# Loading and splitting the first x of a cross-attention kernel in another way, with the bias of the values taken off TensorE and the last pieces put on alternating banks

## The chip, the cores and the metric

The kernel runs on one core of one Trainium2 chip. The metric is the device time in microseconds (us) of one execution. Shown for the kernel before are the median of three runs and one further execution that was profiled.

## What is computed

For each of 32 batches, `x` and `y` (called `ctx_2048` outside) are arrays of 256 channels by 1024 positions in float32; the weights are 256x256. Cut to what matters:

```python
x_q = einsum('oc,bcn->bno', w_qk, y)
x_k = einsum('oc,bcn->bon', w_qk, x)
x_v = einsum('oc,bcn->bon', w_v, x) + b_v[None, :, None]
energy = einsum('bnc,bcm->bnm', x_q, x_k)
attention = softmax(energy, axis=-1)
attention = attention / (1e-07 + attention.sum(axis=1, keepdims=True))
x_r = einsum('bcn,bnm->bcm', x_v, attention)
x_r = relu(einsum('oc,bcn->bon', w_t, x - x_r) + b_t[None, :, None])
return x + x_r
```

## The kernel before, in words

**Arithmetic.** Every large product is made of three products of rounded float32 numbers: an operand is held as a HIGH form, a LOW form and a REST form (`FORMS`, line 210), and a left form is multiplied with its matching right form. So a product for 128 output channels and 512 columns is six matmuls of 128x512 (two blocks of input channels, three forms). Both query and key weights are folded into one matrix `gw` (w_qk times itself), and w_t and w_v into `vw`. So the program first makes `gw` (`square` and `weights`, lines 721 to 752), the transposed w_t (`turn_w`, line 798), from it `tw` and `vw` (`value_weights`, line 820), and a few bias vectors (`biases`, line 827).

**Work of a batch.** `keys` multiplies `gw` with the forms `xf` of x and leaves the forms `gf`; `values` (V) multiplies `vw` with `xf`, turns the result with VectorE into the tile `turned`, sends it through DRAM (`blocks`) and back into `yr` or `turned`, and makes the forms `uf` from it; `straight` (W) multiplies `tw` with `xf` and leaves `xe`; `energy` (E0 to E7) multiplies the forms `yf` of y with `gf`, takes a minimum on VectorE, an exponential on ScalarE, and leaves the forms `ef` and the running sum `acc`; `attention` (A0 to A7) multiplies `uf` with `ef`. The LOW form of `ef` is the last one to be ready: GpSimd adds it up from two parts (line 527). `sums` and `finish` divide, add and store. The last batch has an ending of its own, `ready_end`, `divided`, `beside` and `end` (lines 595 to 673): there W is added into the same banks as the attention, and VectorE takes it out of them in pieces that are stored at once.

**First batch.** x of batch 0 comes into `xr` by four DMAs of 128 partitions by 512 columns (lines 701 and 702), two on SyncE's queue and two on ScalarE's. `first_x(h)` (line 754) makes the forms of one half of the columns: for the first 128 channels ScalarE copies HIGH and VectorE makes REST and LOW; for the other 128 VectorE (first half) or GpSimd (second half) copies HIGH, GpSimd makes REST and VectorE makes LOW. `first_keys` (tokens fH00 and so on: form, block of channels k, half of the columns h) gives two matmuls of the first keys.

**Order.** TensorE's order is written out by hand as strings of tokens (lines 167 to 181): `SET_UP`, `FIRST` for batch 0, `STEADY`, `BEFORE` and `LAST`. In them `z` is one idle product on the tile `few`, `x0` and `x1` a call of `first_x`, G, T, Q and b the four weight steps, y the first two loads of y. The orders of all other engines, and of the DMAs on SyncE's and ScalarE's queues, come out of the class `Plan` (lines 17 to 163). It knows for each operation an engine, a length, a delay, what it reads and writes and whether it holds the SBUF access that VectorE and GpSimd have in common (`port`); it tries four variants (`LOOKS`) of a list schedule and emits that with the shortest span by its own numbers. A changed length or a changed string can so move instructions anywhere in the program. The program waits for a DMA by one of eight lanes taken in turn; a DMA that takes a lane which is still in use waits for it on the engine that issues it.

All computing instructions carry line 231 of the profile, since a helper records them; they are told apart by their tiles.

Of the kernel before, what the change touches and what calls it, by code (L numbers as in the profile page):

```python
# [184 lines left out]
def kernel(  # L185
# [513 lines left out]
    half = [ts(h, MB) for h in range(MH)]  # L699
    load(["wqk0", "wqk1"], 2.7, [(wqk[:, k], w_qk[ts(k, P)]) for k in range(KC)])  # L700
    load(["xr00", "xr10"], 6.0, [(xr[:, k, half[0]], x[0, ts(k, P), half[0]]) for k in range(KC)])
    load(["xr01", "xr11"], 7.4, [(xr[:, k, half[1]], x[0, ts(k, P), half[1]]) for k in range(KC)])
    load(["wt0", "wt1"], 8.3, [(wt[:, k], w_t[ts(k, P)]) for k in range(KC)])
    load(["wv0", "wv1"], 9.2, [(wv[:, k], w_v[ts(k, P)]) for k in range(KC)])
# [245 lines left out]
```

## Time and profile before

| What | Value |
| --- | --- |
| median of three runs | 1937.68 us (1937.02 to 1938.92) |
| the profiled execution's own time | 1936.26 us |
| its span, first to last instruction | 1934.5 us |
| TensorE busy | 1926.5 us, 8500 matmuls |
| VectorE, ScalarE, GpSimd busy | 1493.8, 1474.2, 1549.4 us |
| instructions | 24348 |
| first values product of batch 0 starts | 18.38 us |
| first attention product of batch 0 starts | 40.83 us |

The profiled execution lies 1.76 us over its span and 1.42 us under the median of the runs. PE stands for TensorE's matmuls, PEld for its weight loads, DVE for VectorE, ACT for ScalarE, POOL for GpSimd; SPq and ACTq are instructions that issue a DMA. In a timeline row come the start and the length in us, the engine, the operation with what it writes and reads, the shape, and how many such instructions in a row are merged; in square brackets stands the idle time before them and what ended it. TensorE's matmuls are pipelined: the distance from one start to the next tells their rate, not the length of one.

### The profile page before, as it was taken

What the parts mean: (1) busy time and instruction counts of PE and PEld (TensorE: products, weight loads), DVE (VectorE), ACT (ScalarE), POOL (GpSimd) and SP (SyncE); (2) the same over time, 40 slices, a digit from 0 to 9 for tenths busy, and PEclk for the clock granted to TensorE, in tenths of its full rate; (3) what the DMA queues carried; (4) which work ended last, traced back from release to release, by engine and by line L of the source; (5) the groups of instructions that cost most, each with busy time, mean ns of one, the idle gap of its engine ahead of it and who ended that gap; (6) DMA issues with size and microseconds to landing.
All of it is one profiled execution on the core that took longest, in us unless ns stands there. A gap on an engine that the chain in (4) does not pass through costs nothing.

```text
span 1934.5 us, 24348 instructions
## 1 busy us (share of the span) xinstructions
PE 1926.5 (100%) x8500; PEld 1593.5 (82%) x8500; DVE 1493.8 (77%) x2107; ACT 1474.2 (76%) x1929; POOL 1549.4 (80%) x775
## 2 busy tenths in 40 slices
PE   9999999999999999999999999999999999999998
PEld 7888888888888888888888888888888888888887
DVE  7777787787777877778777777777787777877777
ACT  6778777788777887777977778777787777887775
POOL 5788877888778888787887878877888778887777
PEclk9999999999999999999999999999999999999999
DMA  6675666666666657666575675666656666667642
GB/s 181 141 175 149 177 164 147 147 160 167 173 147 149 160 160 179 144 153 159 157 176 145 149 172 144 184 156 147 156 153 174 167 149 143 162 164 177 158 102 77
DMA packets 128779, 301.76 MB, mean 156 GB/s; under 512 B 12944, under 2 KB 47248, under 8 KB 128656
## 3 DMA queue, kind: packets, MB, share of 16 engines
q1 hardware_dynamic: 92256, 200.19, 33.4%
q0 software_dynamic: 35680, 99.10, 29.2%
q8 instruction: 67, 1.10, 0.2%
q10 hardware_dynamic: 720, 0.92, 0.1%
q14 instruction: 56, 0.46, 0.1%
HBM read 167.25 MB, written 67.11 MB: 121 GB/s over the span
## 4 chain that ended last, share of the span: by engine, by line
PE 99%; DVE 1%; issue 0%; DVEq 0%; ACT 0%
PE banks L231 99%; DVE xf L231 0%; DVE z L231 0%; DVE banks L231 0%; DVE gw L231 0%; DVE xe L231 0%; DVEq L945 0%; ACT gw L231 0%; DVE few L231 0%; DVE nbias L231 0%; DVE ubias L231 0%
## 5 line engine op out<-in xcount | busy, mean ns | idle before, releaser
L231 POOL TENSOR_TENSOR ef<-ef 128x1024 fp32r<-128x1024 f32 x256 | 619.5, 2421 | 140.4 <-DVE acc L231 59.4
L231 PE MATMUL banks<-gf,yf 128*128 128x512 f32 x3072 | 727.6, 389 | 0.0
L231 PE MATMUL banks<-ef,uf 128*128 128x512 f32 x3072 | 727.2, 389 | 0.0
L231 PEld LDWEIGHTS banks<-gf,yf 128*128 128x128 f32 x3072 | 576.3, 188 | 120.7 <-DVE ef L231 0.6
L231 PEld LDWEIGHTS banks<-ef,uf 128*128 128x128 f32 x3072 | 576.8, 188 | 119.6
L231 DVE SCALAR_TENSOR_TENSOR ef<-banks,small,ef 128x512 fp32r<-128x512 f32 x512 | 369.9, 743 | 59.1 <-ACT ef L231 56.9
L231 DVE TENSOR_REDUCE small<-banks 128x1 f32<-128x1024 f32 x256 | 312.2, 1220 | 131.9 <-PE banks L231 131.9
L231 ACT ACTIVATE ef<-banks,small 128x512 fp32r<-128x512 f32 x512 | 337.4, 688 | 12.4 <-DVE acc L231 1.2
L231 ACT ACTIVATE banks<-banks,small 128x1024 f32<-128x1024 f32 x256 | 278.4, 1088 | 81.4 <-DVE small L231 80.8
L231 DVE SCALAR_TENSOR_TENSOR acc<-banks,small,acc 128x512 f32<-128x512 f32 x448 | 317.4, 744 | 5.5
L231 ACT ACTIVATE gf<-banks 128x1024 fp32r<-128x1024 f32 x64 | 65.7, 1029 | 307.3 <-PE banks L231 307.3
L231 ACT ACTIVATE ef<-ef 128x1024 fp32r<-128x1024 f32 x256 | 270.9, 1059 | 1.1
L231 POOL TENSOR_TENSOR z<-z,xe 128x1024 f32<-128x1024 f32 (+1 forms) x64 | 150.8, 2373 | 107.3 <-DVE z L231 104.9
L231 POOL TENSOR_TENSOR uf<-yr,uf 128x1024 fp32r<-128x1024 f32 x64 | 153.6, 2400 | 48.5 <-ACT uf L231 48.5
L231 PE MATMUL banks<-xf,gw 128*128 128x512 f32 x768 | 186.1, 390 | 1.8 <-DVE xf L231 1.7
L231 PE MATMUL banks<-xf,tw 128*128 128x512 f32 (+1 forms) x774 | 184.9, 388 | 0.8 <-DVE z L231 0.6
L231 PE MATMUL banks<-xf,vw 128*128 128x512 f32 x768 | 184.7, 389 | 0.0
L231 PEld LDWEIGHTS banks<-xf,gw 128*128 128x128 f32 x768 | 143.7, 188 | 32.7 <-DVE xf L231 1.5
L231 PEld LDWEIGHTS banks<-xf,tw 128*128 128x128 f32 x774 | 144.6, 188 | 31.1 <-DVE z L231 0.8
L231 PEld LDWEIGHTS banks<-xf,vw 128*128 128x128 f32 x768 | 144.1, 188 | 30.3 <-DVE ef L231 0.3
L231 POOL TENSOR_TENSOR xf<-xr,xf 128x1024 fp32r<-128x1024 f32 (+1 forms) x64 | 151.0, 2382 | 6.2 <-DVE xf L231 6.2
L231 POOL TENSOR_TENSOR uf<-turned,uf 128x1024 fp32r<-128x1024 f32 x64 | 155.2, 2424 | 0.0
(69 smaller groups left out, 1573.3 us busy)
## 6 DMA issues: line engine op xcount, KB each, us to landing
yr<-in_ctx_dram SPq DMA_DIRECT2D x64, 512.0 KB, 3.9
blocks<-turned SPq DMA_DIRECT2D x256, 128.0 KB, 2.7
yf<-in_ctx_dram POOLq DMA_DIRECT2D x63, 512.0 KB, 6.1
yf<-yf POOLq DMA_DIRECT2D x63, 512.0 KB, 6.6
xr<-in_x_dram SPq DMA_DIRECT2D x62, 512.0 KB, 3.8
xo<-in_x_dram SPq DMA_DIRECT2D x62, 512.0 KB, 4.5
xf<-xf POOLq DMA_DIRECT2D x62, 512.0 KB, 5.8
out_dram<-z SPq DMA_DIRECT2D x62, 512.0 KB, 4.5
```

Of the source, the lines that this page charges most:

```text
L231: self.last = getattr(self.engine, name)(*args, **kwargs)
```

## The change

Four things are changed.

1. x of batch 0 is loaded by blocks of 128 channels: each block is two DMAs of 64 partitions by 1024 columns, one on each of the two queues. In both kernels these DMAs are issued between those of w_qk and those of w_t. `first_x(k)` takes a block of channels instead of a half of the columns; ScalarE copies HIGH, and VectorE makes REST and LOW, for both blocks. GpSimd has no part in it any more.
2. The product of w_t and b_v (eight matmul passes with one column, on the path of `biases`) is dropped from TensorE. b_v is loaded into all 128 partitions (128 KB written instead of 1 KB), GpSimd multiplies it with w_t, and VectorE sums the rows up.
3. In `end`, the last block of channels of the last batch is made in four groups of 256 columns that go to the two banks in turn, instead of one of 512 columns and two of 256 on one bank.
4. The strings `SET_UP` and `FIRST` are written anew, some lengths given to the planner too, y's first load gets an earlier due time, and a copy of one column on ScalarE is put ahead, so that ScalarE's table is loaded there.

```diff
 SET_UP = (
-    "x1 z G z z x0 z fH10 y fH00 fR10 T fH01 fL10 b fR01 fR00 fL01 Q fL00 fH11 fL11 fR11"
+    "z z z x0 z G T x1 fH00 fR00 fH01 fR01 fL00 Q fL01 fH11 fH10 fL10 y b fR11 fR10 fL11"
 FIRST = (
-    "V0^ W1^ E0 E1 V1^ W0^ X E2 E3 A0 A1 E4 E5 A2 A3 E6 E7 A4 Y2 A5 Y3 v0 A6 S k0 A7 k1 O"
+    "V0^ V1^ W1^ E0 E1^ W0^ E2 E3 X A0 A1 E4 E5 Y2 A2 A3 E6 E7 A4 Y3 A5 v0 A6 k1 S A7 O k0"
...
-        by_sync(5.8 if q else 7.8, [], ["yr"], lambda: sync.dma_start(r, from_))
+        by_sync(5.8 if q else 7.3, [], ["yr"], lambda: sync.dma_start(r, from_), early=0.0 if q else 45.0)
...
-        for h in range(MH):
-            cuts = [(0, MB)] if not last or h != MH - 1 else [(0, MB // 2), (MB // 2, MB)]
-            for lo, hi in cuts:
+        cuts = [(0, MB)] if not last else [(0, MB // 2), (MB // 2, MB)]
+        for lo, hi in cuts:
+            for h in range(MH):
...
-    load(["xr00", "xr10"], 6.0, [(xr[:, k, half[0]], x[0, ts(k, P), half[0]]) for k in range(KC)])
-    load(["xr01", "xr11"], 7.4, [(xr[:, k, half[1]], x[0, ts(k, P), half[1]]) for k in range(KC)])
+    for k, landing in enumerate((4.4, 5.8)):
+        load(
+            [f"xr{k}0", f"xr{k}1"], landing,
+            [(xr[ts(q, P // 2), k], x[0, k * P + q * (P // 2) : k * P + (q + 1) * (P // 2)]) for q in range(2)],
+        )
...
+    plan.add("act", 1.3, 0.0, ["few"], ["acc0"], lambda: act.copy(acc[:, :1], few[:, :1]), early=59.0)
...
-    def first_x(h):
-        at = ts(h, MB)
-        for k in range(KC):
+    def first_x(k):
+        raw_names = [f"xr{k}{q}" for q in range(2)]
+        for h in range(MH):
...
-                if k == 0:
-                    on_act(MB, [f"xr{k}{h}"], nh, lambda: act.copy(high, raw))
-                elif h == 0:
-                    dve_in_sbuf(MB // 2, [f"xr{k}{h}"], nh, lambda: dve.tensor_copy(high, raw))
-                else:
-                    on_pool(MB // 2, [f"xr{k}{h}"], nh, lambda: pool.tensor_copy(high, raw))
-                add = dve_in_sbuf if k == 0 else on_pool
-                on = dve if k == 0 else pool
-                add(
-                    MB, [f"xr{k}{h}"] + nh, nr,
-                    lambda: on.tensor_tensor(rest, raw, value(high), ALU.subtract),
-                )
+                on_act(MB, raw_names, nh, lambda: act.copy(high, raw))
+                dve_in_sbuf(MB, raw_names + nh, nr, lambda: dve.tensor_tensor(rest, raw, value(high), ALU.subtract))
...
-        by_sync(6.8, [], ["bv"], lambda: sync.dma_start(bv, b_v.rearrange("(k p o) -> p k o", p=P, o=1)))
+        by_sync(6.6, [], ["bv"], lambda: sync.dma_start(bvs, b_v.partition_broadcast(P)))
...
-        plan.add("pe", 0.45, 0.163, ["wtT", "bv", "z1", "acc0", "acc1"], ["wtb", "bank7"], product)
+        on_pool(
+            KC * C, ["wt0", "wt1", "bv", "z0", "z1"], ["wqk0", "wqk1"],
+            lambda: pool.tensor_tensor(each, wt, bvs.unsqueeze(1).broadcast_to([P, KC, C]), ALU.mult),
+        )
 
         def of():
+            dve.tensor_reduce(nbias[:, :, 0], each, AX.X, ALU.add)
```

TensorE's rows at the start of the program before (`few` are the idle products, `z` with 256 columns is G, `z` with 128 columns is T, `xf,gw` are the first keys, `z,acc` is the bias product, `acc,z` is Q, `xf,vw` V, `xf,tw` W, `gf,yf` E):

```order
L231 MATMUL banks<-few 128x128 x6
L231 MATMUL banks<-z 128x256 x4
L231 MATMUL banks<-few 128x128 x3
L231 MATMUL banks<-xf,gw 128x512 x6
L231 MATMUL banks<-z 128x128 x4
L231 MATMUL banks<-xf,gw 128x512 x4
L231 MATMUL banks<-z,acc 128x1 x4
L231 MATMUL banks<-xf,gw 128x512 x6
L231 MATMUL banks<-acc,z 128x256 x4
L231 MATMUL banks<-xf,gw 128x512 x8
L231 MATMUL banks<-xf,vw 128x512 x12
L231 MATMUL banks<-xf,tw 128x512 x12
```

The same place on TensorE now:

```order
L231 MATMUL banks<-few 128x128 x9
L231 MATMUL banks<-z 128x256 x4
L231 MATMUL banks<-z 128x128 x4
L231 MATMUL banks<-xf,gw 128x512 x10
L231 MATMUL banks<-acc,z 128x256 x4
L231 MATMUL banks<-xf,gw 128x512 x14
L231 MATMUL banks<-xf,vw 128x512 x24
L231 MATMUL banks<-xf,tw 128x512 x12
```

All nine idle products now stand ahead of G, T ahead of all 24 matmuls of the first keys, Q behind ten of them, and the second values product (V1) directly behind the first.

VectorE's rows behind the two memsets before, up to the last step of `vw` (`xe<-banks,gw` and `xe<-banks,vw` are intermediate results of `weights`; `xf` are the forms of x):

```order
L231 SCALAR_TENSOR_TENSOR xe<-banks,gw 128x256 x2
L231 SCALAR_TENSOR_TENSOR gw<-banks,gw 128x256
L231 CAST xf<-xr 128x512
L231 SCALAR_TENSOR_TENSOR gw<-banks,gw 128x256
L231 TENSOR_TENSOR xf<-xr,xf 128x512
L231 SCALAR_TENSOR_TENSOR xf<-xf 128x512
L231 TENSOR_TENSOR xf<-xr,xf 128x512
L231 SCALAR_TENSOR_TENSOR xf<-xf 128x512 x2
L231 TENSOR_SCALAR ubias<-banks 128x2
L231 TENSOR_TENSOR nbias<-banks,z 128x2
L231 TENSOR_SCALAR xbias<-nbias 128x2
L231 SCALAR_TENSOR_TENSOR xf<-xf 128x512
```

VectorE's rows there now, with the steps of `vw` that stand between and behind:

```order
L231 TENSOR_TENSOR xf<-xr,xf 128x512
L231 SCALAR_TENSOR_TENSOR xf<-xf 128x512 x2
L231 TENSOR_TENSOR xf<-xr,xf 128x512
L231 SCALAR_TENSOR_TENSOR xe<-banks,gw 128x256
L231 SCALAR_TENSOR_TENSOR xf<-xf 128x512
L231 TENSOR_TENSOR xf<-xr,xf 128x512
L231 SCALAR_TENSOR_TENSOR gw<-banks,gw 128x256
L231 SCALAR_TENSOR_TENSOR xe<-banks,vw 128x256
L231 SCALAR_TENSOR_TENSOR xf<-xf 128x512
L231 SCALAR_TENSOR_TENSOR xe<-banks,vw 128x256
L231 SCALAR_TENSOR_TENSOR vw<-banks,vw 128x256 x2
```

Three rows of `gw` and `xf` stand ahead of these (`xe<-banks,gw`, a TENSOR_TENSOR on `xf`, `gw<-banks,gw`). So VectorE has eight steps on `xf` instead of seven, the steps of `gw` and `vw` stand between them, and the bias rows are gone from here: they follow 4 rows behind, among the steps of `gf`.

VectorE's rows in a batch from the middle of the program, from E0's minimum on (TENSOR_REDUCE on `small`) to the second half of `ef` of E1, before:

```order
L231 TENSOR_REDUCE small<-banks 128x1 x2
L231 RECIPROCAL small<-small 128x1
L231 TENSOR_SCALAR acc<-banks,small 128x512 x2
L231 RECIPROCAL small<-small 128x1
L231 SCALAR_TENSOR_TENSOR ef_80<-banks,small,ef_80 128x512
L231 SCALAR_TENSOR_TENSOR acc<-banks,small,acc 128x512
L231 TENSOR_REDUCE small<-banks 128x1
L231 SCALAR_TENSOR_TENSOR ef_80<-banks,small,ef_80 128x512
L231 SCALAR_TENSOR_TENSOR acc<-banks,small,acc 128x512
L231 SCALAR_TENSOR_TENSOR ef_81<-banks,small,ef_81 128x512
L231 RECIPROCAL small<-small 128x1
L231 SCALAR_TENSOR_TENSOR ef_81<-banks,small,ef_81 128x512
```

The same stretch now:

```order
L231 TENSOR_REDUCE small<-banks 128x1
L231 RECIPROCAL small<-small 128x1
L231 TENSOR_REDUCE small<-banks 128x1
L231 TENSOR_SCALAR acc<-banks,small 128x512 x2
L231 TENSOR_REDUCE small<-banks 128x1
L231 SCALAR_TENSOR_TENSOR ef_80<-banks,small,ef_80 128x512
L231 RECIPROCAL small<-small 128x1
L231 SCALAR_TENSOR_TENSOR ef_80<-banks,small,ef_80 128x512
L231 SCALAR_TENSOR_TENSOR acc<-banks,small,acc 128x512 x2
L231 RECIPROCAL small<-small 128x1
L231 SCALAR_TENSOR_TENSOR ef_81<-banks,small,ef_81 128x512 x2
```

The minimum of E2 has moved ahead of both halves of E0's `ef_80`, and the second reciprocal behind it. Such small exchanges stand in the repeated part of VectorE's, ScalarE's, GpSimd's and SyncE's order (28 batches read alike in each kernel); TensorE's order is the same there.

Three places on the queues belong to the change too. On SyncE's queue, y's first load (512 KB) now stands directly behind w_v and ahead of b_v and b_t, where it stood behind them. On ScalarE's queue the load of its half of w_v stands behind the table load and waits for the lane of a DMA of x's first block; ScalarE's first copy of x stands behind it. GpSimd's first operation of its own is now the step `xe<-acc,tw` of `tw`.

More of the change, by code (lines that the diff above doesn't have):

```diff
@@ L684 @@
     bt = two(3)[:, 0, P : P + KC].rearrange("p (k o) -> p k o", o=1)
-    bv = two(3)[:, 0, P + KC : P + 2 * KC].rearrange("p (k o) -> p k o", o=1)
+    bvs = two(3)[:, 1]
     wtT = acc[:, : KC * C]
@@ L698 @@
     queue = {by_sync: 0, by_act: 0}
[L699 to L704 removed]
+    load(["wqk0", "wqk1"], 2.75, [(wqk[:, k], w_qk[ts(k, P)]) for k in range(KC)])
+    for k, landing in enumerate((4.4, 5.8)):
[3 more added lines that the diff above has]
+        )
+    load(["wt0", "wt1"], 6.5, [(wt[:, k], w_t[ts(k, P)]) for k in range(KC)])
+    load(["wv0", "wv1"], 7.2, [(wv[:, k], w_v[ts(k, P)]) for k in range(KC)])
     plan.add("dve", 0.2, 0.0, [], ["few"], lambda: dve.memset(few, 0.0))
@@ L719, with square @@
     idle_products(5)
-    def square(bank, left, right, reads, writes, blocks_of=lambda w: w):
+    def square(bank, left, right, reads, writes, blocks_of=lambda w: w, busy=(0.87, 0.87)):
         for i in range(KC):
@@ L728, in of @@
                     )
-            fp32_on_pe(KC, C, reads, [writes[i], f"bank{bank + i}"], of)
+            plan.add("pe", busy[i], 0.163, reads, [writes[i], f"bank{bank + i}"], of)
     def weights(to, name, bank, by, d, d_name):
@@ L827, in biases @@
     def biases():
-        by_sync(6.8, [], ["bv"], lambda: sync.dma_start(bv, b_v.rearrange("(k p o) -> p k o", p=P, o=1)))
+        by_sync(6.6, [], ["bv"], lambda: sync.dma_start(bvs, b_v.partition_broadcast(P)))
         by_sync(6.8, [], ["bt"], lambda: sync.dma_start(bt, b_t.rearrange("(k p o) -> p k o", p=P, o=1)))
-        wtb = banks[:, 7, C : C + KC]
-        def product():
-            for i in range(KC):
-                for k in range(KC):
-                    matmul(
-                        wtb[:, i : i + 1], wtT[:, k * C + i * P : k * C + (i + 1) * P], bv[:, k], k == 0, k == KC - 1
-                    )
-        plan.add("pe", 0.45, 0.163, ["wtT", "bv", "z1", "acc0", "acc1"], ["wtb", "bank7"], product)
+        each = two(0)
+        on_pool(
+            KC * C, ["wt0", "wt1", "bv", "z0", "z1"], ["wqk0", "wqk1"],
+            lambda: pool.tensor_tensor(each, wt, bvs.unsqueeze(1).broadcast_to([P, KC, C]), ALU.mult),
+        )
         def of():
-            dve.tensor_scalar(ubias[:, :, 0], wtb, EPS, None, ALU.mult)
-            dve.tensor_tensor(nbias[:, :, 0], wtb, bt[:, :, 0], ALU.subtract)
+            dve.tensor_reduce(nbias[:, :, 0], each, AX.X, ALU.add)
+            dve.tensor_scalar(ubias[:, :, 0], nbias[:, :, 0], EPS, None, ALU.mult)
+            dve.tensor_tensor(nbias[:, :, 0], nbias[:, :, 0], bt[:, :, 0], ALU.subtract)
             dve.tensor_scalar(xbias[:, :, 0], nbias[:, :, 0], -1.0, None, ALU.mult)
-        plan.add("dve", 0.6, 0.0, ["wtb", "bank7", "bt", "z1"], ["bias"], of)
+        plan.add("dve", 1.05, 0.0, ["wqk0", "wqk1", "bt", "z0", "z1"], ["bias"], of, port=1.05)
     def set_up(token):
         if token == "G":
-            square(4, wqk, wqk, ["wqk0", "wqk1", "z0"], [f"gwin{i}" for i in range(KC)])
+            square(4, wqk, wqk, ["wqk0", "wqk1", "z0"], [f"gwin{i}" for i in range(KC)], busy=(1.95, 1.3))
             weights(gw, "gw", 4, -UP, work[:, : KC * C], "gwd")
```

3 lines of the change are left out of this document (2 added, 1 removed).

## The prediction

> **What bounds the kernel now.** I read the page first, then its group of the commonest matmul, the chain that ended last, and a table by stretches (start and end, length, then busy us and instructions of PE, PEld, DVE, ACT, POOL).
>
> ```profile
> span 1934.5 us, 24348 instructions
> L231 PE MATMUL banks<-gf,yf 128*128 128x512 f32 x3072 | 727.6, 389 | 0.0
> 9.23 2.79 DVE xf L231 x2
> 13.63 1.76 DVE xf L231
> 35.26 1890.36 PE banks L231 x8337
> 1928.86 1.74 DVE z L231 x3
> 40.83:1925.00 1884.17, 1884.17 (x8313) 1560.07 (x8312) 1460.24 (x2060) 1448.16 (x1892) 1525.77 (x754) 1.00 0.63 156
> ```
>
> TensorE is the bound. The 3072 matmuls of the commonest form had no idle time in front of them, the chain lies on PE from 35.26 us on, and PE is busy in all of 40.83 to 1925. That work is not touched: the same matmuls at the same rate. What can be won lies ahead of 40.83 and behind 1925. In the set-up the chain goes over VectorE's forms of x (4.6 us in the two rows), at the end over its last pieces.
>
> **The set-up: TensorE's own path.** First TensorE and the loads it waits for (PE and ACTq rows of the timeline; then DMA issues with KB and median us to landing, x's first one alone and both together):
>
> ```profile
> 9.38 0.60 PE L231 MATMUL banks<-z 128*128 128x128 f32 x4
> 14.34 1.03 PE L231 MATMUL banks<-acc,z 128*128 128x256 f32 x4
> 18.38 2.88 PE L231 MATMUL banks<-xf,vw 128*128 128x512 f32 x12
> 21.10 2.88 PE L231 MATMUL banks<-xf,tw 128*128 128x512 f32 x12
> 1.17 0.93 ACTq L231 DMA_DIRECT2D xr<-in_x_dram  x2
> 2.13 0.45 ACTq L231 DMA_DIRECT2D z<-in_L_xattn_w_t_dram  x1
> 3.59 0.33 ACTq L231 DMA_DIRECT2D z<-in_L_xattn_w_v_dram  x1
> xr<-in_x_dram ACTq DMA_DIRECT2D x1, 256.0 KB, 4.8
> xr<-in_x_dram ACTq DMA_DIRECT2D x2, 256.0 KB, 5.1
> z<-in_L_xattn_w_t_dram ACTq DMA_DIRECT2D x1, 128.0 KB, 5.9
> z<-in_L_xattn_w_v_dram ACTq DMA_DIRECT2D x1, 128.0 KB, 5.0
> ```
>
> Twelve matmuls of 512 columns take 2.72 us from start to start (18.38 to 21.10). After the change TensorE starts T when w_t has landed, 2.13 + 5.9 = 8.0 us: the loads in front of it are the same bytes in the same place, so "in front of w_t" is nothing new. Then come T (0.6), the 24 matmuls of the first keys (5.44) and Q (two runs of four passes; 1.03 less the tail of the last one, about 0.87 each: 1.73). Nothing in the way, the first values product would start at 8.0 + 0.6 + 5.4 + 1.7 = 15.8 us, with hand-overs 15.9, against 18.38 now. The bias product goes from this path, the idle products are as many as before and only move ahead of G; G ends later for that, which the wait for w_t covers.
>
> Of the loads behind, y enters SyncE's queue about 3 us earlier, behind everything that the set-up needs there, so it delays only b_v, b_t and what follows, which are due much later. ScalarE's half of w_v, issued at 3.59 now, must wait for x's first block, which I expect where the first half of x lands now, at 1.17 + 4.8 = 6.0; with 5.0 us to land, a figure from a fuller queue, it is there by 11.0. Q comes at 8.0 + 0.6 + ten matmuls (2.27) = 10.9. No charge, a few tenths in the range.
>
> **The set-up: VectorE's path.**
>
> ```profile
> 7.07 1.12 ACT L231 CAST xf<-xr 128x512 fp32r<-128x512 f32 x2
> 6.63 0.41 DVE L231 SCALAR_TENSOR_TENSOR gw<-banks,gw 128x256 fp32r<-128x256 f32 x1
> 10.24 1.77 DVE L231 TENSOR_TENSOR xf<-xr,xf 128x512 fp32r<-128x512 f32 x1
> 12.04 3.35 DVE L231 SCALAR_TENSOR_TENSOR xf<-xf 128x512 fp32r<-128x512 f32 x2
> 15.64 0.69 DVE L231 SCALAR_TENSOR_TENSOR xf<-xf 128x512 fp32r<-128x512 f32 x1
> 16.24 0.42 DVE L231 SCALAR_TENSOR_TENSOR xe<-banks,vw 128x256 f32<-128x256 f32 x1
> 9.86 1.60 POOL L231 TENSOR_TENSOR xf<-xr,xf 128x512 fp32r<-128x512 f32 x1
> 11.43 1.73 POOL L231 TENSOR_TENSOR xe<-acc,tw 128x512 f32<-128x512 f32 x1
> ```
>
> A step on `xf` costs VectorE 0.69 alone, 0.60 to the next start (15.64 to 16.24), but 1.7 beside GpSimd. Its ends tell why: the step of 10.24 ends at 12.01, 0.55 behind the end of GpSimd's 9.86 + 1.60, and the chain's next one starts at 13.63, 0.5 behind GpSimd's 11.43 + 1.73. Each waits until GpSimd's instruction is over. Steps that read a bank and one tile (0.41) show no such wait.
>
> The change takes three GpSimd steps of x away. VectorE's new queue up to the end of `vw` is eight `xf` steps (8 x 0.60 = 4.8) and eight of `gw` and `vw` (8 x 0.40 = 3.2): 8.0 us. It starts when ScalarE has issued w_v (6.0 + 0.33), copied one half of x (1.12 for two, 0.5 each) and made the first HIGH of `gw` (estimated as long as the DVE row of that size, 0.4): 7.25. That would be 15.25 with no wait at all. Two GpSimd steps, `xe<-acc,tw` and y's first, come while VectorE is still at `xf`; each can cost what a step beside GpSimd costs more than one alone, 1.77 - 0.69 = 1.1. I take one, since VectorE's steps on banks lie between and can hide the other: 16.35, bounds 15.25 (then TensorE's 15.9 holds) and 17.5. The values product needs the last step of `vw` for its fourth matmul, so it starts at 16.4 on TensorE: 2.0 us earlier than 18.38.
>
> [...] The new loads give one half of the partitions to each queue, and both queues run at once, so I charge nothing; the case is a rival below.
>
> **The first batch.** From the first values product to A0 stand eight products in both kernels (before V W E E V W E E), 8 x 2.72 = 21.8.
>
> ```profile
> 40.83 3.34 PE L231 MATMUL banks<-ef,uf 128*128 128x512 f32 x14
> 21.30 1.25 DVE L231 STREAM_TRANSPOSE turned<-banks 128x1024 f32<-128x1024 f32 x1 [0.56 <-PE banks L231]
> 40.05 4.75 POOL L231 TENSOR_TENSOR ef<-ef 128x1024 fp32r<-128x1024 f32 x2
> 24.02 1.12 ACT L231 ACTIVATE xe<-banks,xbias 128x1024 f32<-128x1024 f32 x1 [0.56 <-PE banks L231]
> 26.09 3.27 PEld L231 LDWEIGHTS banks<-gf,yf 128*128 128x128 f32 x15 [0.40 <-DVE gf L231]
> 22.57 1.79 SPq L231 DMA_DIRECT2D blocks<-turned  x4
> 27.82 0.34 SPq L231 DMA_DIRECT2D yr<-blocks  x1
> ```
>
> Now 18.38 + 21.8 = 40.1, so 0.7 is lost in waits ahead of 40.83. If none is left, A0 would start at 16.4 + 21.8 = 38.2, 2.6 earlier. But its last third, from 1.81 on, needs `ef` of E0 from GpSimd. That ends at 40.05 + 2.37 = 42.4 now, just ahead of 40.83 + 1.81 = 42.6, and it hangs on the way of the first values: turned at 21.30, through DRAM, two GpSimd steps on `uf`, then `ef`. This way moves by V0's 2.0 us, to 40.4 against the 40.0 at which TensorE would be there: 0.4 waited. ScalarE's order now has an eviction (1.12) in front of the step between the two on `uf`, so up to 1.5. I charge 0.8. The second values product, now directly behind the first, waits in its banks for the four block DMAs (22.57 to 27.82: 5.3 us) before VectorE may overwrite `turned`; from 20.6 that is 25.9, plus 1.25 for turning = 27.1, and E1 wants the banks at 16.4 + 4 x 2.72 = 27.3. No charge, 0.5 at worst.
>
> The bias step on VectorE (a reduction of 512 columns and three small ones, about 1.2) stands ahead of the last `gf` form. E0's last third waits for that form until 26.09 now; it moves 2.0 earlier with the keys and 1.2 later with the bias, to 25.3, and is needed at 16.4 + 3 x 2.72 + 1.81 = 26.4. Hidden, with 1.1 to spare.
>
> Sum through A0: 2.6 - 0.8 = 1.8 us saved, bounds 0.6 and 2.6.
>
> **The end.**
>
> ```profile
> 1925.64 1.44 DVE L231 SCALAR_TENSOR_TENSOR banks<-banks,ubias,rc 128x512 f32<-128x512 f32 x2 [0.38 <-PE banks L231]
> 1929.40 0.98 PE L231 MATMUL banks<-xf,tw 128*128 128x256 f32 x6 [0.58 <-DVE z L231]
> 1929.92 0.68 DVE L231 SCALAR_TENSOR_TENSOR z<-z,xr 128x512 f32<-128x512 f32 x1
> 1930.51 0.48 DVE L231 SCALAR_TENSOR_TENSOR z<-banks,nbias,xr 128x256 f32<-128x256 f32 x1
> ```
>
> TensorE's 0.58 goes, since the next group is in the other bank. But VectorE is late next. One division of the first channels (0.7) now stands ahead of the two in the banks, so TensorE begins about 0.3 later. The first division ends at 1925.64 + 0.3 + 0.75 = 1926.7, two groups of six matmuls at 0.12 and a tail of 0.2 make 1928.3. From there VectorE has five steps, a piece of 0.48, two of 0.6 and two more pieces of 0.45: about 2.6, to 1930.9, against 1930.51 + 0.48 = 1930.99 now. I take nothing; bounds 0.5 better, 0.3 worse.
>
> **The sum.** 1.8 us against the profiled execution: 1934.5 - 1.8 = 1932.7 span, 1936.26 - 1.8 = 1934.5 of its own time. The runs' median lies 1.4 above that execution, at 1937.68, and I give the same distance: 1935.9 us. About 0.2% (3.9 us) is what a measurement of this kernel can tell from no change, so this forecast is "same", below 1937.68.
>
> **The rivals.** (a) GpSimd and the late w_v cost VectorE both collisions: V0 at 17.5, 0.9 earlier, less a few tenths for the exchanged eviction: saved 0.6, 1937.1 us. For it, every `xf` step beside GpSimd collided before; against it, GpSimd has less to do there. 18%.
>
> (b) The half-partition loads run at half the rate. Priced by rows: the first block lands at 6.0 and the second, issued near 1.6 and 5.4 under way (the mean of both is 5.1), at 7.0 us; that is 1.0 for a block at full flow, so half the rate puts w_t 2.0 later at 10.0 and V0, by TensorE's path, at 17.9. Saved 0.5 less the POOL charge, about 0.2: 1937.5. [...] 8%.
>
> (c) Everything on TensorE's path: V0 at 15.9 (2.5), the 0.7 of waits gone, 0.5 at the end and w_t 0.3 earlier through larger pieces: 4.0 saved, 1933.7. Against it, the POOL row at 40.05 must move just as far. 8%.
>
> (d) Slower: the exchanged steps in the middle batches make a wait that returns.
>
> ```profile
> 695.40 0.74 DVE L231 SCALAR_TENSOR_TENSOR ef<-banks,small,ef 128x512 fp32r<-128x512 f32 x1
> 696.06 0.16 DVE L231 RECIPROCAL small<-small 128x1 f32<-128x1 f32 x1
> 696.51 2.88 PE L231 MATMUL banks<-gf,yf 128*128 128x512 f32 x12
> ```
>
> E3 takes E1's banks at 696.51, VectorE left the first of them at 696.14: 0.37 to spare. With E2's minimum and one reciprocal (0.16) in front, 0.2 is left. From 0.35 of further delay on, 28 batches pay over 0.14 each and 3.9 in all; with 0.3 each it is 8.4 less 1.8 saved: 1944.3 us. Against it, VectorE has 23% of the time free to catch up, and the two bank halves are needed 1.36 apart. 7%.
>
> **How the numbers follow.** The forecast has 59%: 1934.9 to 1937.0. (a) and (b) lie just above it, still inside 0.2%. Faster by over 0.2%: (c), 8%. Slower: (d), 7%. Same: 85%. The range 1933.6 to 1938.2 takes in (a), (b), most of (c) and half a microsecond of spread between medians, and leaves out (d).
>
> **What would show it.** Right: the first `xf,vw` matmul at 16.4 (15.9 to 17.5), `xf` steps of VectorE at 0.6 to 0.7 except one or two behind a POOL row, A0 near 39, a wait of TensorE on POOL `ef` inside A0, last VectorE piece at its old distance from the last attention matmul. Wrong would be V0 later than 17.5 (the step on VectorE's queue fails), A0 gaining as much as V0 plus 0.7 (the POOL charge fails), or PE waits that come back in every batch.

## The result, and the profile after

| | before | after |
| --- | --- | --- |
| median of the runs | 1938.02 us (1936.98 to 1939.45, 8 runs) | 1944.59 us (1941.66 to 1945.98, 8 runs) |
| the profiled execution, its span | 1936.26, 1934.5 us | 1944.83, 1942.4 us |

The ratio of after to before is 1.0032 (95% interval 1.0021 to 1.0042): 6.6 us slower in the medians, where 1.8 us less was forecast. The spread has grown too, from 2.5 to 4.3 us. First the page's group of the commonest matmul:

```profile
L231 PE MATMUL banks<-gf,yf 128*128 128x512 f32 x3072 | 728.2, 389 | 2.0 <-DVE ef L231 1.1
```

This matmul, which had no idle time in front of it before, now has 2.0 us. TensorE's timeline after, at the places that matter:

```profile
9.23 0.63 PE L231 MATMUL banks<-z 128*128 128x128 f32 x4 [2.53 <-DMA z<-in_L_xattn_w_t_dram]
20.35 0.73 PE L231 MATMUL banks<-xf,gw 128*128 128x512 f32 x2 [3.50 <-DVE xf L231]
21.02 3.32 PE L231 MATMUL banks<-xf,vw 128*128 128x512 f32 x8
34.69 1.65 PE L231 MATMUL banks<-gf,yf 128*128 128x512 f32 x6 [0.89 <-DVE turned L231]
45.70 2.68 PE L231 MATMUL banks<-ef,uf 128*128 128x512 f32 x9
1859.59 1.65 PE L231 MATMUL banks<-gf,yf 128*128 128x512 f32 x6 [0.89 <-DVE ef L231]
1929.03 5.60 PE L231 MATMUL banks<-ef,uf 128*128 128x512 f32 x24
```

and the row of before that answers to the last of these:

```profile
1920.68 5.60 PE L231 MATMUL banks<-ef,uf 128*128 128x512 f32 x24
```

These starts cut both spans into four pieces: to the first values product (V0), on to the first attention product (A0), on to the last attention product, and the end. Before they are 18.38, 22.45, 1879.85 and 13.82; after 21.02, 24.68, 1883.33 and 13.37. So 2.6 us are lost ahead of V0, 2.2 between V0 and A0, 3.5 in the long piece that I took to be untouched, and 0.45 is won at the end: 7.9 in all.

What happened ahead of V0 stands in VectorE's and GpSimd's rows after:

```profile
12.11 1.44 DVE L231 SCALAR_TENSOR_TENSOR xf<-xf 128x512 fp32r<-128x512 f32 x1
13.47 1.78 DVE L231 TENSOR_TENSOR xf<-xr,xf 128x512 fp32r<-128x512 f32 x1
15.84 4.46 DVE L231 SCALAR_TENSOR_TENSOR xf<-xf 128x512 fp32r<-128x512 f32 x1
...
11.50 1.50 POOL L231 TENSOR_TENSOR xe<-acc,tw 128x512 f32<-128x512 f32 x1 [10.19 <-ACT tw L231]
12.96 1.74 POOL L231 TENSOR_TENSOR yf<-yr,yf 128x512 fp32r<-128x512 f32 x1
15.57 1.74 POOL L231 TENSOR_TENSOR tw<-acc,tw 128x512 fp32r<-128x512 f32 x1
17.03 1.50 POOL L231 TENSOR_TENSOR yf<-yf 128x512 fp32r<-128x512 f32 x1
18.25 1.49 POOL L231 TENSOR_TENSOR z<-z 128x512 f32<-128x512 f32 x1
```

The step of 12.11 waits out one GpSimd instruction: it ends at 13.55, 0.55 behind 11.50 + 1.50. The step of 13.47 does the same with the next (12.96 + 1.74). The step of 15.84, the last on the first x, waits out three: it ends at 20.30, 0.56 behind 18.25 + 1.49. The third, `z<-z`, is the new product of w_t and b_v. TensorE has nothing to do for 3.50 us, and then (a table by stretches: start and end, length, busy us of PE, PEld, DVE, ACT, POOL, granted clock, DMA share, GB/s)

```profile
18.18:21.59 3.41, 1.24 (x4) 0.78 (x5) 3.21 (x4) 0.92 (x3) 1.56 (x2) 1.00 1.03 274
21.59:25.00 3.41, 3.41 (x10) 2.63 (x9) 1.22 (x1) 3.38 (x5) 1.20 (x1) 0.50 0.30 47
```

its clock is granted at 0.50 for 3.41 us: the matmuls come every 0.427 us instead of 0.227. The 24 matmuls from V0 on take 7.18 us (the next product starts at 28.20) instead of 5.44, so 1.7 us are lost.

### The profile page after: what moved, and what is told of

It is laid out like the page before. It is cut to its first block, busy times and chain, and to the rows that moved or that the text cites. A ratio compares the mean times of both kernels' runs of the same rounds, so it can differ in the third digit from the quotient of the medians.

```text
span 1942.4 us, 24357 instructions
## 1 busy us (share of the span) xinstructions
PE 1928.4 (99%) x8498; PEld 1593.4 (82%) x8498; DVE 1498.3 (77%) x2110; ACT 1462.5 (75%) x1932; POOL 1549.7 (80%) x773
## 4 chain that ended last, share of the span: by engine, by line
PE 93%; ACT 3%; DVE 2%; DMA 2%; issue 1%; SPq 0%; POOL 0%; DVEq 0%; ACTq 0%
PE banks L231 93%; ACT ef L231 1%; DMA blocks<-turned 1%; ACT banks L231 1%; DMA yr<-blocks 1%; DVE xf L231 1%; SPq L231 0%; DMA xr<-in_x_dram 0%; ACT yf L231 0%; DVE ef L231 0%; ACT uf L231 0%; DVE acc L231 0%; DVE turned L231 0%; ACT xf L231 0%; DVE small L231 0%
## 5 line engine op out<-in xcount | busy, mean ns | idle before, releaser
L231 POOL TENSOR_TENSOR ef<-ef 128x1024 fp32r<-128x1024 f32 x256 | 630.3, 2463 | 83.0 <-ACT ef L231 47.4
L231 DVE SCALAR_TENSOR_TENSOR ef<-banks,small,ef 128x512 fp32r<-128x512 f32 x512 | 360.8, 740 | 8.1 <-ACT ef L231 4.8
L231 ACT ACTIVATE ef<-banks,small 128x512 fp32r<-128x512 f32 x512 | 330.2, 700 | 8.2 <-DVE acc L231 8.1
L231 ACT ACTIVATE ef<-ef 128x1024 fp32r<-128x1024 f32 x256 | 276.3, 1080 | 2.3
L231 POOL TENSOR_TENSOR uf<-turned,uf 128x1024 fp32r<-128x1024 f32 x64 | 168.8, 2638 | 0.5 <-ACT uf L231 0.5
L231 DVE RECIPROCAL small<-small 128x1 f32<-128x1 f32 x256 | 41.3, 161 | 162.4 <-ACT banks L231 162.2
```

What stands on the lines that cost most here:

```text
L231: self.last = getattr(self.engine, name)(*args, **kwargs)
```

## The experiments

Three theories. **A:** GpSimd's instructions in a row hold VectorE off, and the idle time that this makes costs TensorE its full rate. **B:** the loads into 64 partitions set the start. **C:** the planner chose another of its four variants (the first, where it took the third for the kernel before), and that order makes new waits all over the program.

All runs in one table. V0 to "end" are read from the profiled execution of each as above. The intervals are against runs of the kernel before that were measured together with each; in the experiments their medians were 1937.43 to 1937.97.

| run | variant | median us (runs) | ratio, 95% interval | V0 | V0 to A0 | A0 to last | end |
| --- | --- | --- | --- | --- | --- | --- | --- |
| before | 3 | 1938.02 (8) | 1 | 18.38 | 22.45 | 1879.85 | 13.82 |
| after | 1 | 1944.59 (8) | 1.0021 to 1.0042 | 21.02 | 24.68 | 1883.33 | 13.37 |
| a_bias | 1 | 1943.61 (6) | 1.0018 to 1.0041 | 20.93 | 24.66 | 1882.48 | 13.33 |
| a_pool | 1 | 1941.66 (11) | 1.0006 to 1.0025 | 19.16 | 23.00 | 1883.91 | 14.83 |
| a_load | 1 | 1943.74 (7) | 1.0017 to 1.0039 | 19.90 | 24.62 | 1883.77 | 14.31 |
| a_warm | 1 | 1943.82 (7) | 1.0019 to 1.0041 | 20.57 | 23.52 | 1882.43 | 13.38 |
| b_look | 1 | 1943.93 (5) | 1.0023 to 1.0049 | 19.15 | 24.16 | 1884.29 | 13.30 |
| a_look | 3 | 1939.37 (11) | 1.0008 to 1.0025 | 17.31 | 23.68 | 1880.79 | 13.72 |
| b_end | 3 | 1938.10 (11) | 0.9993 to 1.0011 | 18.99 | 22.20 | 1880.97 | 13.74 |
| a_pw | 1 | 1939.11 (11) | 1.0001 to 1.0018 | 18.93 | 23.11 | 1883.16 | 13.40 |
| mix_c | 3 | 1936.97 (11) | 0.9987 to 1.0004 | 16.57 | 23.84 | 1880.86 | 13.73 |
| mix_e | 3 | 1937.81 (11) | 0.9991 to 1.0010 | 18.40 | 24.17 | 1881.24 | 13.69 |
| mix_d | 3 | 1937.64 (11) | 0.9992 to 1.0009 | 16.67 | 26.01 | 1880.41 | 13.71 |
| mix_f | 3 | 1935.60 (11) | 0.9981 to 0.9999 | 16.04 | 23.36 | 1880.63 | 13.77 |

In every experiment the planner is pinned to the variant named in the table. The longer ends of a_pool and a_load were not followed up.

**a_bias: a need more for the new product.**

```diff
-            KC * C, ["wt0", "wt1", "bv", "z0", "z1"], ["wqk0", "wqk1"],
+            KC * C, ["wt0", "wt1", "bv", "z0", "z1", "xf111"], ["wqk0", "wqk1"],
```

> The changed kernel, with one more thing that GpSimd's product of w_t and b_v waits for: the last step of VectorE on the first x. Nothing else moves on any engine. Theory A (VectorE's last step was held off by three GpSimd steps in a row, the third of them this product): the step ends 1.2 earlier, near 19.1 instead of 20.30, the first values product starts near 19.8 instead of 21.02, TensorE's idle time is 2.3 instead of 3.5 and so perhaps too short for the half rate that followed (another 1.75): 2.9 us in all, about 1941.7, or 1.2 alone (1943.4) if the half rate stays. Theory B (the slower loads of the first x set the start, the GpSimd steps only fill the wait): nothing moves, 1944.6. Theory C (the waits in the last two batches make the loss): nothing moves either.

The need stands only in the planner's list, and it changed no row on any engine; nothing in the program waits for it. So this is the changed kernel once more, and it tells nothing of the theories. As a repeat it tells that two medians of the same program lie 1.0 us apart.

**a_pool: three GpSimd steps later.** The same need also at the first step of y and at the last of `tw`; here the planner's order does change, and GpSimd's rows behind `xe<-acc,tw` become `tw`, the issue of y's DMA, `yf<-yr,yf`, `z<-z`, `yf<-yf`.

```diff
-                    columns, ["yr"] + nh, nr,
+                    columns, ["yr", "xf111"] + nh, nr,
...
-            KC * C, ["wtT", "acc0", "acc1"] + names[LOW], names[REST],
+            KC * C, ["wtT", "acc0", "acc1", "xf111"] + names[LOW], names[REST],
```

> The changed kernel, with three GpSimd steps behind VectorE's last step on the first x: the product of w_t and b_v, the last step of tw and the first step of y. One GpSimd step of tw stays in front. Theory A (GpSimd holds VectorE off): the last step of the first x needs 0.7 instead of 4.5, the first values product starts at 17.1 to 17.6, where TensorE's own path from w_t puts it (9.2 + 0.6 + 5.4 + 1.7 = 17.0), with no half rate behind it: 3.6 + 1.75 = 5.3 us less than the changed kernel, about 1939.3. If GpSimd's steps come too late for the first W or E0 behind it, up to 1 us is given back. Theory B (the loads): the first values product does not come ahead of 20, under 1 us less. Theory C: nothing.

VectorE's last step, GpSimd's neighbours of it, and TensorE in a_pool's timeline:

```profile
16.93 0.68 DVE L231 SCALAR_TENSOR_TENSOR xf<-xf 128x512 fp32r<-128x512 f32 x1
...
14.23 1.54 POOL L231 TENSOR_TENSOR tw<-acc,tw 128x512 fp32r<-128x512 f32 x1 [0.74 <-ACT tw L231]
18.32 1.75 POOL L231 TENSOR_TENSOR yf<-yr,yf 128x512 fp32r<-128x512 f32 x1
...
9.90 0.63 PE L231 MATMUL banks<-z 128*128 128x128 f32 x4 [3.36 <-DMA z<-in_L_xattn_w_t_dram]
10.28 4.00 PE L231 MATMUL banks<-xf,gw 128*128 128x512 f32 x10
14.07 2.06 PE L231 MATMUL banks<-acc,z 128*128 128x256 f32 x8
19.16 5.15 PE L231 MATMUL banks<-xf,vw 128*128 128x512 f32 x22
```

With no GpSimd instruction beside it the step takes 0.68 instead of 4.46, and the wait of 3.50 is gone: the first half of A is shown. The median falls by 2.9 us where 5.3 was expected. V0 is at 19.16 and not at 17.1 to 17.6, since w_t landed late in this execution and the half rate came here instead: ten matmuls took 3.79 (10.28 to 14.07) instead of 2.27, at a mean granted clock of 0.62 from 9.90 to 14.30.

**a_load: the same loads in 128 partitions.**

```diff
-            [(xr[ts(q, P // 2), k], x[0, k * P + q * (P // 2) : k * P + (q + 1) * (P // 2)]) for q in range(2)],
+            [(xr[:, k, ts(q, MB)], x[0, ts(k, P), ts(q, MB)]) for q in range(2)],
```

> The changed kernel, with each block of the first x loaded as two pieces of 128 partitions by 512 columns instead of two of 64 partitions by 1024; queues, bytes and their order stay. Theory A: the loads land up to 1.1 earlier (first block near 6.0 instead of 7.1, w_t's product at 8.1 instead of 9.2), but the start of the first values product hangs on how GpSimd's steps meet VectorE's: between 18 and 20.5, so 0.5 to 4 us less. Theory B (half-partition loads set the start): it starts 1.1 earlier, at 19.9, and 1.1 to 2.9 us are saved. If the partitions make no difference to a load, both landings stay where they are and the time stays at 1944.6.

ScalarE's first copy of x and TensorE's T in a_load:

```profile
5.36 0.62 ACT L231 CAST xf<-xr 128x512 fp32r<-128x512 f32 x1 [1.25 <-DMA xr<-in_x_dram]
...
8.08 0.66 PE L231 MATMUL banks<-z 128*128 128x128 f32 x4 [1.39 <-DMA z<-in_L_xattn_w_t_dram]
```

The same copy after:

```profile
7.16 0.62 ACT L231 CAST xf<-xr 128x512 fp32r<-128x512 f32 x1 [2.65 <-DMA xr<-in_x_dram]
```

In this pair the half-partition loads cost 1.8 us at x and 1.15 at w_t (9.23 - 8.08). Landings differ between executions: that copy starts at 6.41 to 7.65 in the six profiles with half-partition loads and at 5.31 to 6.58 in the five with loads into 128 partitions (a_load and the mixtures below), 1.1 apart on average. T waits for w_t until 9.13 to 9.90 in the six; in the mixtures it starts at 8.25 to 8.93 with 0.2 us of waiting at most. VectorE's last step was still held (14.34, 4.50 in the chain), and V0 came 1.1 earlier, as B has it, but only to 19.90, and the median fell by 0.85, less than the 1.1 to 2.9 expected under B. The loads are a part of the loss, not its cause.

**a_warm: idle products in the wait.**

```diff
                 matmul(pair(i)[:, h], gw[:, j, k, ts(i, P)], xf[:, j, k, ts(h, MB)], start, stop)
+            if (j, k, h) == (REST, 1, 0):
+                for _ in range(12):
+                    pe.matmul(banks[:, 4, :P], few, few, start=True, stop=True)
```

> The changed kernel, with 12 idle products of 128x128 on TensorE in front of the two matmuls that wait for the last step of the first x, in a bank that is free; the other engines' orders stay. Theory A: the first values product still starts at 21.0, but TensorE has idled for under 1 us instead of 3.5, its next ten matmuls come at 0.227 instead of 0.427, and the time falls by 1.75 us to 1942.8. If the half rate does not come from the idle time, nothing changes: 1944.6.

```profile
16.35 2.84 PE L231 MATMUL banks<-few 128*128 128x128 f32 x24
19.90 0.73 PE L231 MATMUL banks<-xf,gw 128*128 128x512 f32 x2 [0.71 <-DVE xf L231]
20.57 3.73 PE L231 MATMUL banks<-xf,vw 128*128 128x512 f32 x15
```

V0 runs at the full rate (granted clock 1.00 from 20.57 to 23.60), and V0 to A0 is 1.2 shorter than after. The median shows nothing of it: 1943.82, against 1944.59 and 1943.61 for the changed kernel. In its runs the mean granted clock lies between 0.998 and 1.000, so the half rate may have come at other places in some. The profile agrees with A; the gain in time is not shown.

**b_look: the kernel before in the variant of the changed one.**

```diff
-            if best is None or self.span < best[0]:
+            if turn == 0:
```

> The kernel before, with the planner made to take the first of its four variants (the one that it takes for the changed kernel) instead of the third; strings, loads and set-up steps stay, and the first rows of every engine too. Theory C (the exchanged order makes the waits near the end and in batches 0 and 1): the first values product stays at 18.4, TensorE gets some 3 us of waits between 70 and 30 us from the end and up to 1 us in the first two batches, none in the batches between: 1938.0 + 2.6 to 1938.0 + 3.6, so 1940.6 to 1941.6. Rival (these waits come from the new strings, loads or end): 1938.0, no change.

1943.93 us, over the 1940.6 to 1941.6 expected: the variant alone makes the kernel before as slow as the changed one. Its profile is its fastest run (1942.86, at the full clock); two of its five took 1946.54 and 1947.91, at a mean granted clock of 0.998. Two waits of TensorE in b_look, then VectorE's rows ahead of the second:

```profile
38.23 1.65 PE L231 MATMUL banks<-gf,yf 128*128 128x512 f32 x6 [0.87 <-DVE ef L231]
1858.04 1.66 PE L231 MATMUL banks<-gf,yf 128*128 128x512 f32 x6 [0.89 <-DVE ef L231]
...
1853.82 0.16 DVE L231 RECIPROCAL small<-small 128x1 f32<-128x1 f32 x1 [2.07 <-ACT banks L231]
1854.46 1.23 DVE L231 TENSOR_REDUCE small<-banks 128x1 f32<-128x1024 f32 x1 [0.48 <-PE banks L231]
1855.61 1.40 DVE L231 SCALAR_TENSOR_TENSOR acc<-banks,small,acc 128x512 f32<-128x512 f32 x2
1857.23 0.75 DVE L231 SCALAR_TENSOR_TENSOR ef<-banks,small,ef 128x512 fp32r<-128x512 f32 x1 [0.23 <-ACT ef L231]
```

The same place in the kernel before:

```profile
1847.63 0.16 DVE L231 RECIPROCAL small<-small 128x1 f32<-128x1 f32 x1 [0.95 <-ACT banks L231]
1847.83 1.41 DVE L231 SCALAR_TENSOR_TENSOR acc<-banks,small,acc 128x512 f32<-128x512 f32 x2
1850.00 1.23 DVE L231 TENSOR_REDUCE small<-banks 128x1 f32<-128x1024 f32 x1 [0.77 <-PE banks L231]
1852.52 4.73 PE L231 MATMUL banks<-gf,yf 128*128 128x512 f32 x20
```

Before, `acc` follows 0.2 behind the reciprocal. In b_look the minimum of the next energy stands between them, and VectorE waits 0.48 for TensorE's product before it can take it: `acc` comes 1.8 behind. From it hang `ef` and the freeing of the bank, so TensorE waits 0.89. It is the kind of exchange that rival (d) priced, a minimum ahead of the `acc` and `ef` steps. In the repeated batches TensorE hardly waits for it; in the first 102 us and in the last 85, where other strings set its order, it does. In the changed kernel, counted from A0, the same matmuls start 1.10 later than before at 106.80, 1.14 later at 1855.81 and 3.48 later at the last attention product. TensorE's printed waits in this piece add up to 1.5 of that (0.21, 0.89, 0.23 and 0.20); the rest lies in the same two places, in matmuls that start further apart without a printed wait. The table says the same of all fourteen: A0 to the last attention product is 1882.4 to 1884.3 in variant 1 and 1879.9 to 1881.2 in variant 3, whatever else was changed.

**a_look: the changed kernel in the third variant.**

```diff
-            if best is None or self.span < best[0]:
+            if turn == 2:
```

> The changed kernel, with the planner made to take its third variant, as it does for the kernel before. Theory C: the 2.9 us of waits near the end shrink to 0.4, about 2.5 us less than the changed kernel, 1941.6 or so. The start may move as well, since in this variant GpSimd's product of w_t and b_v stands two places earlier and the bias steps of VectorE directly behind vw: 1.5 us to either side, so 1940.1 to 1943.1. Rival (the waits do not come from the variant): 1944, within 1.

1939.37, better than expected: the long piece is 2.5 shorter, and the start has moved with it. In this variant `z<-z` ends ahead of VectorE's last step on x, which takes 0.68, and V0 starts at 17.31. So this run doesn't separate A from C; b_look does. With both, the four medians make a square: the third variant takes 1937.43 before (measured together with these runs) and 1939.37 after the change, the first 1943.93 and 1944.59. The variant is worth 6.5 and 5.2 us, the rest of the change 1.9 in the third variant and 0.7 in the first, which is less than the 1.0 between two medians of one program. Three of a_look's eleven runs took 1944.23 to 1945.56, at a mean granted clock of 0.997 to 0.998; the other eight lie at 1938.03 to 1941.31, at 0.999 to 1.000. Another VectorE step is held off behind (VectorE, then GpSimd):

```profile
17.58 3.47 DVE L231 TENSOR_TENSOR nbias<-nbias,z 128x2 f32<-128x2 f32 x1
...
18.03 1.75 POOL L231 TENSOR_TENSOR tw<-acc,tw 128x512 fp32r<-128x512 f32 x1
19.29 1.74 POOL L231 TENSOR_TENSOR yf<-yf 128x512 fp32r<-128x512 f32 x1
```

A step on two columns takes 3.47 beside two GpSimd instructions, and V0's turning stands behind it.

**b_end: the third part of the change alone,** in the kernel before.

```diff
-        for h in range(MH):
-            cuts = [(0, MB)] if not last or h != MH - 1 else [(0, MB // 2), (MB // 2, MB)]
-            for lo, hi in cuts:
+        cuts = [(0, MB)] if not last else [(0, MB // 2), (MB // 2, MB)]
+        for lo, hi in cuts:
+            for h in range(MH):
```

> The kernel before with the third part of the change alone: the last pieces in four groups of 256 columns on alternating banks, the planner on the variant of the kernel before. In the changed kernel the last attention product stood 13.37 before the end of the span, in the kernel before 13.82. So 0.45 us less, 1937.5, if that is the work of the four groups; 1938.0 if the difference is chance.

1938.10, ratio 1.0002: no effect, and the end is 13.74 long against 13.82. The 13.37 after belongs to variant 1 (13.30 in b_look, with the old end).

**a_pw: a_pool and six idle products behind G.**

```diff
+                if (bank, i) == (4, KC - 1):
+                    for _ in range(6):
+                        pe.matmul(banks[:, 7, :P], few, few, start=True, stop=True)
```

> The run with three GpSimd steps behind VectorE's last step on x, and six idle products on TensorE between G and T besides. In that run's profile w_t's half came late (T at 9.90, 3.36 us idle) and TensorE's next 16 or so matmuls and passes went at 0.427 instead of 0.227. Theory A with the idle time as the cause of the half rate: T follows on less than 1.9 us of idle time in every run, the first values product starts at 17.1 to 18 instead of 19.2, and the median falls by 1 to 1.5 us to 1940.4, with less spread. If the half rate is no matter of idle time, 1941.7 stays.

1939.11: 2.6 less than a_pool and with a little less spread (4.3 against 4.9 us), more than expected; the intervals of the two overlap. But the profiled execution shows the half rate all the same, behind only 1.51 and 0.22 us of idle time (TensorE's rows, then the table by stretches):

```profile
9.24 0.30 PE L231 MATMUL banks<-z 128*128 128x128 f32 x1 [1.51 <-DMA z<-in_L_xattn_w_t_dram]
9.76 0.55 PE L231 MATMUL banks<-z 128*128 128x128 f32 x3 [0.22 <-DMA z<-in_L_xattn_w_t_dram]
...
7.30:10.71 3.41, 1.68 (x11) 1.24 (x11) 2.47 (x5) 3.40 (x8) 0.00 (x0) 1.00 1.01 308
10.71:14.12 3.41, 3.41 (x10) 2.63 (x9) 3.41 (x6) 2.77 (x5) 1.67 (x2) 0.50 0.45 158
```

So the length of one idle time alone does not decide it, and what the six products did in the median is not shown.

**The mixtures.** mix_c is the changed kernel in variant 3 with a_load's loads, a_pw's six products, the bias steps planned behind the forms of `tw` and of the first keys (token b at the end of `SET_UP`), and the old string `FIRST`. mix_e adds a_pool's two needs; mix_d is mix_c with the new `FIRST`; mix_f exchanges two DMAs of mix_c. mix_c's lines that are new:

```diff
-            KC * C, ["wt0", "wt1", "bv", "z0", "z1"], ["wqk0", "wqk1"],
+            KC * C, ["wt0", "wt1", "bv", "z0", "z1"] + ["tw20", "tw21"], ["wqk0", "wqk1"],
...
-        plan.add("dve", 1.05, 0.0, ["wqk0", "wqk1", "bt", "z0", "z1"], ["bias"], of, port=1.05)
+        plan.add("dve", 1.05, 0.0, ["wqk0", "wqk1", "bt", "z0", "z1"] + ["gf20"], ["bias"], of, port=1.05)
```

> A mixture: the changed kernel with the planner on its third variant, the first x loaded in pieces of 128 partitions, six idle products between G and T, the bias steps of GpSimd and VectorE moved behind the forms of tw and of the first keys, and the first batch's old string (the second values product behind E1). Theory (variant 6 us, set-up 1 to 3 us, no half rate): the waits in the last batches are 0.4, the first values product starts at 16.5 if VectorE's last step on x meets one GpSimd step, at 18.5 if it meets two in a row; the first batch waits 1; the end gives 0.4. So 0.4 to 2.4 less than the kernel before, 1935.5 to 1937.5. Rival (what is won at the start is given back behind it, since GpSimd's steps on uf and ef do not move with it): 1938.

> The mixture, and besides the last step of tw and the first of y on GpSimd are planned behind VectorE's last step on x. As the mixture, but that step of VectorE meets at most one GpSimd step, so the first values product starts at 15.9 to 16.8; y's forms come 2 to 3 us later than in the mixture and E0 may wait up to 1 for them. 1935.3 to 1936.8. Rival (given back behind it): 1938.

> The mixture with the first batch's new string (the second values product directly behind the first). If the second one's turning waits for the block DMAs of the first as in the changed kernel, E1 waits 0.8 to 1.3 more than in the mixture, so 1 us longer than it: 1936.5 to 1938.5. If the wait only came from the late start, no difference.

mix_c starts V0 at 16.57, the time of my forecast, and is 0.6 faster than the kernel before, within its interval. Most of the 1.8 won at the start is given back: A0 is only 0.4 earlier. mix_e gains nothing by its later GpSimd steps: three earlier steps of VectorE on x met a GpSimd step each instead (1.77, 1.77 and 1.76 us), and V0 is at 18.40. mix_d's V0 to A0 is 2.2 longer than mix_c's (half rate is a part of that in its profile: the mean granted clock is 0.86 from 33 to 42), its median 0.7 longer. Where mix_c gives it back: ScalarE, TensorE, the issue on SyncE's queue, and the row of the DMA issues (KB, us to landing) of mix_c:

```profile
32.36 1.05 ACT L231 CAST uf<-yr 128x1024 fp32r<-128x1024 f32 x1 [1.87 <-DMA yr<-blocks]
34.84 5.73 PE L231 MATMUL banks<-gf,yf 128*128 128x512 f32 x24 [1.41 <-DVE ef L231]
22.93 0.46 SPq L231 DMA_DIRECT2D xo<-in_x_dram  x1
25.30 0.34 SPq L231 DMA_DIRECT2D yr<-blocks  x1
...
yr<-blocks SPq DMA_DIRECT2D x1, 512.0 KB, 7.0
```

The first values are back from DRAM at 32.3, 7.0 after the issue (4.9 before); ScalarE waits for them with E0's exponentials queued behind, and E2 waits for E0's bank. The load of `xo` stands in front on the queue. mix_f makes the planner put it behind:

```diff
-        by_sync(4.5, ["blocks"], [name], lambda: sync.dma_start(back, blocks))
+        by_sync(
+            4.5, ["blocks"], [name] + (["back"] if b == q == 0 else []), lambda: sync.dma_start(back, blocks)
+        )
...
-                by_sync(5.2, ["bias"], ["xo"], lambda: sync.dma_start(xo, x[b, ts(c, P)]))
+                by_sync(
+                    5.2, ["bias"] + (["back"] if b == c == 0 else []), ["xo"],
+                    lambda: sync.dma_start(xo, x[b, ts(c, P)]),
+                )
```

> The mixture with two neighbouring DMAs of SyncE's queue exchanged: the first batch's load of xo (512 KB) stands behind the load that brings the first values back from DRAM, instead of in front. In the mixture that load took 7.0 us to land (4.9 in the kernel before), ScalarE's copy of it held up E0's exponentials, and E2 waited 1.8. Theory (the way of the first values through DRAM takes back what the start wins, and the load in front lengthens it): it lands 5 to 6 us after its issue, E2 waits 0.3 to 1, and the median falls by 0.8 to 1.5 from the mixture's 1936.97, to 1935.5 to 1936.2, which is below the kernel before by more than the measurement is uncertain. If the y loads on GpSimd's queue are what slows it, it stays at 7 us and 1937.0.

```profile
30.05 1.04 ACT L231 CAST uf<-yr 128x1024 fp32r<-128x1024 f32 x1
39.40 5.60 PE L231 MATMUL banks<-ef,uf 128*128 128x512 f32 x24
24.78 0.34 SPq L231 DMA_DIRECT2D yr<-blocks  x1
25.17 0.42 SPq L231 DMA_DIRECT2D xo<-in_x_dram  x1
...
yr<-blocks SPq DMA_DIRECT2D x1, 512.0 KB, 3.8
```

The load of the first values lands in 3.8, ScalarE no longer waits for it, A0 starts at 39.40 (40.41 in mix_c), and the median is 1935.60 against 1937.43 of the kernel before: ratio 0.9990 (0.9981 to 0.9999), faster than both kernels by a small margin. Its 11 runs lie within 1.1 us. About half of the 1.0 at A0 is not the exchange's: V0 itself is 0.53 earlier than in mix_c, though no order ahead of it differs. There TensorE's G, from the same start, took 1.85 us (5.06 to 6.91) against 2.54 (5.05 to 7.59).

## Why the prediction was wrong

**"That work is not touched."** This step failed first, at the start of the prediction. The matmuls between A0 and the last attention are the same, but the other engines' order around them is not, and it came from another variant of the planner. The exchange was seen and priced as rival (d), at 7% and as a wait that returns in 28 batches, 8.4 us. The mechanism was right and the place wrong: it costs next to nothing there, and 2.6 to 4.4 us near both ends in the seven profiles of the first variant. That the 1944.3 us of rival (d) lie 0.3 from the measured median is luck: its wait in 28 batches did not come. I took the repeated batches for the whole, and did not ask what the exchange does where other strings set the order. b_look alone, 6.5 us over the kernel before, would have made the forecast "slower".

**VectorE's path.** V0 was forecast at 16.4, at most 17.5, and came at 21.02. The failed step is "I take one": one collision, at 1.1. Three came, at 0.8, 1.1 and 3.8, together 5.6. The two GpSimd steps that I counted both collided, and a collision is not bounded by one GpSimd instruction: the last step met three and cost 3.8 (4.46 - 0.68). I left out the last step of `tw`, `yf<-yf` and the new product, which stood ready one behind the other. VectorE also began at 8.10 and not at 7.25, since x landed later. In the four runs of the changed set-up where at most one step on x is held and the clock stays full, V0 starts at 16.04 to 17.31 (mix_f, mix_c, mix_d, a_look; the first three with x in loads of 128 partitions and later bias steps); in a_pool and a_pw, where the half rate came ahead of it, at 19.16 and 18.93.

The SBUF access in common (`port`) is the planner's model: in it a VectorE step waits until the GpSimd step under way is over, and then goes ahead of the next one. The trace agrees for the step of 12.11, which ended 0.55 behind GpSimd's, and shows more at 15.84, where the waiting step was passed over twice, by the GpSimd instructions of 17.03 and 18.25. The step on a bank at 11.77, `xe<-banks,gw`, took 0.42 beside the GpSimd instruction of 11.50.

**TensorE's path and the loads.** w_t was to land at 8.0; T ran at 9.23. The step "I charge nothing" for the 64 partitions failed by 1.2 us, and a_load gives back 1.15 of them. Rival (b) had the direction, with a price of 2.0, at 8%. That such a load runs at half the rate, from which that price came, is shown by no run; what the runs show is w_t's product 1.15 later (after against a_load) and x's first copy 1.1 later on average. Nor does a run show the 0.3 that rival (c) counted on from larger pieces.

**The half rate** was in none of my cases. It cost 1.7 us in the profile after (granted clock 0.50 from 21.59 to 25.00), and in b_look and a_look the runs at a lower mean clock (0.998, and 0.997 to 0.998) are the long ones.

**The first batch.** "No charge, 0.5 at worst" for V1's turning was too small: E1 waited 0.89 for `turned` and cost 1.2 from start to start, since the four block DMAs of V0 took longer, 6.5 us from their issue (26.94 to 33.39, when VectorE could go on) where I had 5.3. The charge of 0.8 for the way of the first values had the right mechanism and was less than half of the price: in mix_c, with V0 where I had it, V0 to A0 takes 23.84, 2.0 more than the 21.8 of the eight products. mix_f, where the load in front is gone, gets 0.5 of that back (23.36).

**The end.** Taken as nothing, and nothing it was (b_end).

Put together for the profiled execution: 2.6 for V0 where -2.0 was forecast, 2.2 to A0 (1.7 of half rate and 1.2 at E1, less 0.7 of the old waits), 3.5 behind, -0.45 at the end.

## What to carry to other kernels

Where a planner sets the order, its choice among variants is a part of every change: pin it while something else is measured, and look at the batches that differ from the repeated one. A VectorE step with its operands in SBUF is to be priced, at worst, against the whole run of GpSimd instructions that stand ready beside it, not against one: here the same step took 4.46 us beside three and 0.68 beside none. Time won at the start arrives only if the slowest way behind it, here through DRAM and back, moves as well.
